# Two graph layers on one core: the first four chunks' source rows gathered from x before the branch, a shorter last chunk, and a rewritten end of layer 1

## The chip, the cores and the metric

The kernel runs on one core of one Trainium2 chip. The metric is the device time of one execution, in microseconds, as the median of several runs; smaller is better. A profile of one execution comes with it: the span from its first to its last instruction, and a trace of every instruction and transfer.

A core has five instruction streams that work side by side. PE is the matrix engine, DVE the vector engine, ACT the scalar engine with its tables of functions, POOL is GpSimd, and SP only issues transfers. Each works through its own instructions in order and waits at semaphores for the others. Transfers are issued by SP, ACT or GpSimd and carried by 16 DMA engines that they share.

## The reference, cut to what matters

There are 12,500 nodes with rows of 128 numbers and 200,000 edges sorted by their target `dst`. Two layers follow one another. Both gather a row per edge by `src` and add up per target node.

```python
# layer 1: attention with 4 heads of 32
loops = jnp.arange(N); src, dst = edges with the loops appended
xl = (x @ W_l).reshape(N, HEADS, C)
xr = (x @ W_r).reshape(N, HEADS, C)
h = xl[src] + xr[dst]
e = jnp.einsum('ehc,hc->eh', jax.nn.leaky_relu(h, NEG_SLOPE), att)
p = jnp.exp(e - segment_max(e, dst)[dst])
alpha = p / segment_sum(p, dst)[dst]
out = segment_sum(alpha[:, :, None] * xl[src], dst).reshape(N, HID) + bias + x
out = layernorm(out) * ln_gamma + ln_beta
x = layernorm(x + out)
# layer 2
m = x[src] + edge_attr_128
h = 2.0 * x + segment_sum(m, dst)
h = h @ W1 + b1
h = jnp.where(h > 0, h, 0.01 * h)
x = layernorm(x + h @ W2 + b2)
```

## The kernel before, in words

Edges are handled in 112 chunks of 1792, laid out as 128 partitions by T = 14 edges; a column of 128 edges is called a tile here. The last chunk holds the 1088 edges that are left, laid out in the same 14 columns on 78 partitions. As the edges are sorted, the targets of a chunk lie within 128 consecutive nodes, and a chunk's result is 128 node rows; a row that two chunks share is carried from one to the next.

**Prologue** (lines 49 to 136). The index data are loaded (`dsth`, `n0b`, `srcs`), DVE derives from them what the chunks need (`rel`, `same`, `lastf`, `thru`, `nid`, `khot`) and the flag that says whether the sorted path may be used. In 14 groups of 7 node tiles, PE turns the rows of x (L129) and multiplies them by W_l (L134), and `xl = x @ W_l` is written to DRAM as `xl_d`. Then each engine reads the flag and branches (L138, L139). All that follows is inside the branch.

**Layer 1** (`fast_path`, L215 to L601) is written out by hand: under `manual_schedule` the order of the calls is the order on each engine. Iteration c of the loop at L512 holds pieces of four chunks at once: the loads of chunk c+2 (`load0`), the gather and node work of chunk c+1 (`gather`, `nodes1` to `nodes3`, `parts2`, `parts3`, `node_by_edge`), the attention scores of chunk c (`products`, `leaky`, `scores`, `weights0`, `weights1`), the weights, messages and sums of chunk c-1 (`weights2` to `weights6`, `edge_by_node0`, `messages`, `sums`), the merge with the row carried over for chunk c-2 (`merge1`, `merge2`), and the carry of chunk c-3. The two layer norms work on pairs of chunks: `norm1a` and `roots` in odd iterations, `norm1b` and `norm2` in even ones; `norm2` stores the finished rows to `x1_d` (L500). Two more iterations and four more calls after the loop bring the last chunks to their end.

`gather` (L179) issues one indirect transfer per tile on GpSimd:

```python
got = pool.tile([P, T, D], F32, name="got", bufs=4)
...
nc.gpsimd.indirect_dma_start(out=got[:n, t, :], in_=table[:N, :], in_offset=...srcs[:n, c, t:t + 1]...)
```

It reads `xl_d` in layer 1 and `x1_d` in layer 2. There are four buffers, so gather c+1 waits until the messages of chunk c-3, the last readers of its buffer, are through. `products` turns the gathered rows (L302) and adds the target's part (L305); `messages` reads them again (L403).

**Layer 2** (L604 to L693) loads the edge features (`load1`), gathers from `x1_d`, builds a 0/1 matrix on ACT (`edges1`, L198, L199) and multiplies it with both (`sums1`, L633, L634); `finish1` does the dense part and the last norm for up to four chunks and stores the rows.

## Time and profile before

| | us |
|---|---|
| median of 3 runs (4065.29 to 4066.28) | 4066.21 |
| the profiled execution | 4072.12 |
| its span, first to last instruction | 4070.3 |
| PE busy | 3228.6 (79%) |
| GpSimd busy, 3136 gathers (L186) and 5 others | 2991.6 (73%) |
| DVE busy | 1820.0 (45%) |
| ACT busy | 1825.0 (45%) |
| mean granted clock of PE | 0.781 |

On the page, a row of digits shows an engine's busy share in 40 equal slices of the span, in tenths. A group's line gives the line of the kernel, the engine, the operation, what it writes and reads, how often, then its busy time and the mean length of one, then the idle time of the engine just ahead of it and what ended most of it; "issue" means that nothing in the trace was waited for. In a list of waits the columns are the total, the number of times and the longest. A timeline line gives the start and length in us. "POOLq" and "SPq" are the sequencers that issue.

### The profile page before, as it was taken

Reading aid. Unit: us, or ns where it says so; the run is one execution under the profiler, and the core shown is the slowest. Engines: PE = TensorE matmul, PEld = TensorE weight load, DVE = VectorE, ACT = ScalarE, POOL = GpSimd, SP = SyncE. Lnnn points to the kernel's source line nnn. Section 1 sums busy time; section 2 is a strip of 40 time slices with the busy share of each in tenths; the row PEclk is TensorE's granted clock in tenths of the full one; section 3 lists DMA queues with packets and bytes.
Section 4 is the critical chain, followed back from the end, with each engine's and each line's share of the span. In section 5 each row is a group of like instructions: output and inputs, shape, how many; then the busy total and the mean of one; then the engine's idle time right before and its main releaser. Section 6 shows DMA issues by size and latency. Waiting matters only on the chain. (4 is left out here: it accounts for less than half of the span.)

```text
span 4070.3 us, 55444 instructions
## 1 busy us (share of the span) xinstructions
PE 3228.6 (79%) x18162; PEld 2678.9 (66%) x18274; DVE 1820.0 (45%) x6070; ACT 1825.0 (45%) x4382; POOL 2991.6 (73%) x3141
## 2 busy tenths in 40 slices
PE   6988989999898988989857677767767776677776
PEld 5777777777777777777755555555555555555555
DVE  3778787887878878778730101010101001010101
ACT  2555555555555555555543433333333434333332
POOL 2777777777777777777747777777777777777776
PEclk8888887888888888888876777777777777767777
DMA  6334343333334334334323433333333333333332
GB/s 209 105 111 115 115 115 105 115 115 105 114 115 115 115 105 115 110 111 115 103 79 100 121 101 112 110 112 109 95 118 101 121 100 117 105 112 110 102 111 70
DMA packets 236135, 451.21 MB, mean 111 GB/s; under 512 B 66104, under 2 KB 124601, under 8 KB 235836
## 3 DMA queue, kind: packets, MB, share of 16 engines
q0 software_dynamic: 100384, 205.04, 19.4%
q1 hardware_dynamic: 134876, 240.68, 17.6%
q8 instruction: 147, 2.41, 0.2%
q10 hardware_dynamic: 576, 1.84, 0.1%
q14 instruction: 152, 1.25, 0.1%
HBM read 426.22 MB, written 21.10 MB: 110 GB/s over the span
## 5 line engine op out<-in xcount | busy, mean ns | idle before, releaser
L186 POOL DMA_INDIRECT got<-xl_d,srcs x1568 | 1501.9, 958 | 540.9 <-issue 488.4
L186 POOL DMA_INDIRECT got<-x_d,srcs x1568 | 1488.5, 949 | 521.1 <-issue 468.0
L634 PE MATMUL ps<-got,od 128*128 128x128 f32 x3136 | 858.2, 365 | 433.5 <-DMA got<-x_d,srcs 428.1
L634 PEld LDWEIGHTS ps<-got,od 128*128 128x128 f32 x3136 | 629.6, 249 | 578.8 <-DMA got<-x_d,srcs 575.5
L633 PE MATMUL ps<-ea,od 128*128 128x128 f32 x3136 | 782.3, 341 | 18.3 <-DMA ea<-in_edge_attr 18.3
L639 DVE SCALAR_TENSOR_TENSOR h<-x1w,ps 128x128 f32<-128x128 f32 x112 | 32.2, 287 | 1560.0 <-PE ps L634 1560.0
L633 PEld LDWEIGHTS ps<-ea,od 128*128 128x128 f32 x3136 | 640.4, 253 | 44.3 <-issue 25.7
L411 PE MATMUL ps<-val,od 128*128 128x137 f32 x3136 | 586.7, 367 | 6.1 <-DVE val L403 6.1
L411 PEld LDWEIGHTS ps<-val,od 128*128 128x128 f32 x3136 | 568.9, 271 | 6.2 <-issue 5.2
L329 PEld LDWEIGHTS sc<-attm,lk 128*128 128x128 f32 x3136 | 443.3, 213 | 86.5 <-DVE lk L313 65.1
L198 ACT ACTIVATE od<-iota,nrel 128x128 f32<-128x128 f32 x1568 | 479.9, 387 | 0.0
L329 PE MATMUL sc<-attm,lk 128*128 128x4 f32 x3136 | 446.8, 263 | 23.4 <-DVE lk L313 12.2
L644 ACT COPY ns<-ps 128x128 f32<-128x128 f32 x111 | 29.5, 266 | 950.8 <-DVE h L639 950.8
L312 ACT ACTIVATE lk<-ph 128x512 f32<-128x512 f32 x448 | 242.7, 542 | 356.6 <-PE ph L305 355.2
L313 DVE TENSOR_TENSOR lk<-ph,lk 128x512 f32<-128x512 f32 x448 | 278.3, 621 | 231.1 <-ACT lk L312 229.4
L305 PE MATMUL ph<-odt,parts 128*128 128x512 bf16 (+1 forms) x1232 | 320.2, 366 | 7.9 <-ACT odt L295 1.7
L302 PE MATMUL ph<-ident,got 128*128 128x128 f32 x1568 | 279.1, 290 | 48.0 <-DMA got<-xl_d,srcs 47.3
L319 DVE TENSOR_TENSOR od<-bank,rel 128x512 f32<-128x512 f32 x448 | 272.1, 608 | 60.7 <-PE ps L411 60.6
L403 DVE TENSOR_TENSOR val<-got,bank 128x512 f32<-128x512 f32 x448 | 274.0, 613 | 0.9 <-issue 0.5
L302 PEld LDWEIGHTS ph<-ident,got 128*128 128x128 f32 x1568 | 198.8, 155 | 108.9 <-DMA got<-xl_d,srcs 54.3
L293 ACT ACTIVATE odt<-row,nnid 128x1024 bf16<-128x1024 int32 x224 | 233.6, 1043 | 0.0
L199 ACT ACTIVATE od<-od 128x896 f32<-128x896 f32 x224 | 212.7, 949 | 7.1
(142 smaller groups left out, 3253.8 us busy)
## 6 DMA issues: line engine op xcount, KB each, us to landing
ea<-in_edge_attr SPq DMA_DIRECT2D x111, 896.0 KB
row<-in_dst_rows SPq DMA_DIRECT2D x336, 256.0 KB
got<-xl_d,srcs POOLq DMA_INDIRECT x1568
got<-x_d,srcs POOLq DMA_INDIRECT x1568
row<-in_dst_rows SPq DMA_DIRECT2D x112, 128.0 KB
xg<-in_x_pad SPq DMA_DIRECT2D x112, 64.0 KB
x_d<-x1w SPq DMA_DIRECT2D x112, 64.0 KB
out<-y SPq DMA_DIRECT2D x111, 64.0 KB
```

Of the source, the lines that this page charges most:

```text
L186: nc.gpsimd.indirect_dma_start(out=got[:n, t, :], out_offset=None, in_=table[:N, :], in_offset=bass.IndirectOffsetOnAxis(ap=srcs[:n, c, t: ...
L198: nc.scalar.activation(od[:, t, :], iota[:, 0, :], AF.Abs, bias=nrel[:, c, t:t + 1])
L302: nc.tensor.matmul(ph[:, t * P:(t + 1) * P], got[:, t0 + t, :], ident, start=(t == 0), stop=False, is_transpose=True)
L305: nc.tensor.matmul(ph[:, :m * P], parts[:, k, :], odt[:, t0 * P:(t0 + m) * P], start=False, stop=(k == 2))
L312: nc.scalar.mul(lk[:, :m * P], ph[:, :m * P], 0.2)
L313: nc.vector.tensor_max(lk[:, :m * P], ph[:, :m * P], lk[:, :m * P])
L319: nc.vector.tensor_tensor(live["od", c][:, t0:t0 + m, :], bank[:, None, :P].to_broadcast([P, m, P]), rel[:, c, t0:t0 + m, None].to_broadca ...
L329: nc.tensor.matmul(live["sc", c][:, :, t0 + t], lk[:, t * P:(t + 1) * P], attm, start=True, stop=True)
L403: nc.vector.tensor_mul(vh[:, :, :, :C], live["got", c][:, t0:t0 + m, :].rearrange("p t (h c) -> p t h c", h=H), wts[:, t0:t0 + m, :, None] ...
L411: nc.tensor.matmul(ps, od[:, t, :], v[:, t, :], start=(t == 0), stop=(t == T - 1))
L633: nc.tensor.matmul(ps, od[:, t, :], ea[:, t, :], start=(t == 0), stop=False)
L634: nc.tensor.matmul(ps, od[:, t, :], got[:, t, :], start=False, stop=(t == T - 1))
```

## The change

Six things change; the path that is taken when the flag is 0 is also touched, for memory, and does not run here.

1. Constants `EARLY = 4` and `RING = 6`. The gathered rows live in a ring of six fixed buffers instead of four from a pool. `gather` moves into the prologue's function; chunks 0 to 3 are gathered there, ahead of all else, from x instead of `xl_d`. Their `srcs` columns are loaded first.
2. After the branch, `project` turns those four chunks' rows tile by tile and multiplies them by W_l in place: chunk 0 before the loop, chunks 1 to 3 at the end of iterations 0 to 2.
3. The constants of `fast_path` are loaded in the prologue (`constants`), DVE's preparation is spread over the prologue's groups (`later`), and the prologue's turn and multiply steps are interleaved with one step's distance. The row data of chunks 0 and 1 are loaded in one piece each on ACT's queue.
4. The last chunk has 9 tiles on 121 partitions; `tiles[c]` replaces T in the steps of a chunk.
5. The loop of layer 1 ends with iteration 110. What followed is written out anew in another order, with the 0/1 matrix of the last chunk built on ACT in a free buffer of the ring, `sums` of chunk 110 in two parts, and `norm1a`, `norm1b` and `norm2` of the last pairs partly on GpSimd. The last pair is split into two single chunks.
6. `roots` does not load the exponential's table again at the very end.

```diff
+EARLY = 4
+RING = 6
...
+    tiles = [T] * (NCH - 1) + [-(-(E - (NCH - 1) * CE) // P)]
...
+    nc.scalar.dma_start(srcs[:, :1], src_of[:, :1])
+    nc.scalar.dma_start(srcs[:, 1:EARLY], src_of[:, 1:EARLY])
+    ring = [const.tile([P, T, D], F32, name=f"got{i}") for i in range(EARLY)]
+
+    def gather(table, c):
+        got = ring[c % RING]
+        n = min(P, -(-(E - c * CE) // tiles[c]))
+        if n < P:
+            nc.vector.memset(got[n // 32 * 32:, :tiles[c]], 0.0)
+        for t in range(tiles[c]):
+            nc.gpsimd.indirect_dma_start(
+                out=got[:n, t, :], out_offset=None, in_=table[:N, :],
+                in_offset=bass.IndirectOffsetOnAxis(ap=srcs[:n, c, t:t + 1], axis=0))
+        return got
+
+    for c in range(EARLY):
+        gather(a["x_pad"], c)
...
+        def constants():
+            nc.sync.dma_start(n0i, a["n0_row"])
+            nc.sync.dma_start(iota[:, 0, :], a["c_iota"][:, :P].to_broadcast([P, P]))
...
+        def later(i):
+            if i == 0:
+                nc.vector.tensor_scalar(khot, kd, pcol, None, op0=OP.is_equal)
...
+            elif i == 1:
+                nc.vector.memset(same[:, :, 0:1], 0.0)
+                constants()
+                nc.vector.tensor_tensor(same[:, :, 1:], dstf[:, :, :S - 1], dstf[:, :, 1:],
+                                        op=OP.is_equal)
...
+            elif i == 4:
+                nc.vector.tensor_scalar(nrel, rel, -1.0, -FAR, op0=OP.mult, op1=OP.max)
...
+        turn(*parts[0])
+        for i in range(1, len(parts)):
+            turn(*parts[i])
+            times(*parts[i - 1])
+        times(*parts[-1])
...
+    ring += [cp.tile([P, T, D], F32, name=f"got{i}") for i in range(EARLY, RING)]
...
+        pairs = [(c, 2) for c in range(0, NCH - 2, 2)]
+        pairs += [(c, 1) for c in range(2 * len(pairs), NCH)]
...
+            if c < 2:
+                nc.scalar.dma_start(row, a["dst_rows"][c:c + 1, :].to_broadcast([P, CE]))
...
+        def project(c):
+            got, xTs = live["got", c], {}
+
+            def turn(q):
+                t0, m = quads[c][q]
+                pT = ep.tile([P, 4 * P], F32, name="pm", bufs=2)
+                for t in range(m):
+                    nc.tensor.transpose(pT[:, t * P:(t + 1) * P], got[:, t0 + t, :], ident)
+                xTs[q] = ew.tile([P, 4 * P], F32, name="lk", bufs=3)
+                nc.scalar.copy(xTs[q][:, :m * P], pT[:, :m * P])
+
+            def times(q):
+                t0, m = quads[c][q]
+                pl = ep.tile([P, 4 * P], F32, name="ph", bufs=2)
+                for t in range(m):
+                    nc.tensor.matmul(pl[:, t * P:(t + 1) * P], xTs[q][:, t * P:(t + 1) * P],
+                                     wlr[:, 0, :], start=True, stop=True)
+                nc.vector.tensor_copy(got[:, t0:t0 + m, :].rearrange("p t d -> p (t d)"),
+                                      pl[:, :m * P])
...
         load0(0)
         load0(1)
-        put("got", 0, gather(ew, xl_d, 0))
+        for c in range(EARLY):
+            put("got", c, ring[c])
+        project(0)
         nodes1(0)
         nodes2(0)
+        node_by_edge(0, 0, 0)
+        node_by_edge(0, 0, 1)
         parts2(0)
         parts3(0)
         nodes3(0)
...
-        for c in range(NCH + 2):
+        for c in range(NCH - 1):
...
-            if nxt:
-                put("got", c + 1, gather(ew, xl_d, c + 1))
+            if c + 1 >= EARLY:
+                put("got", c + 1, gather(xl_d, c + 1))
...
+            if c + 1 < EARLY:
+                project(c + 1)
...
+        c, k = NCH - 1, len(pairs) - 1
+        weights2(c - 1)
+        edge_by_node0(c - 1, 0)
+        edge_by_node0(c - 1, 1)
+        carry(c - 3)
+        weights3(c - 1)
+        edge_by_node0(c - 1, 2)
+        products(c, 0)
+        weights4(c - 1)
+        merge1(c - 2)
+        leaky(c, 0)
+        weights5(c - 1)
+        weights6(c - 1)
+        edge_by_node0(c - 1, 3)
+        merge2(c - 2)
+        messages(c - 1, 0)
+        messages(c - 1, 1)
+        products(c, 1)
+        scores(c, 0)
+        leaky(c, 1)
+        messages(c - 1, 2)
+        messages(c - 1, 3)
+        put("od", c, ring[(c + 1) % RING])
+        edge_by_node(live["od", c], c, 0, tiles[c])
+        products(c, 2)
+        scores(c, 1)
+        leaky(c, 2)
+        scores(c, 2)
+        weights0(c)
+        weights1(c)
+        norm1a(k - 2, pool)
+        roots(k - 2)
+        weights2(c)
+        sums(c - 1, 0, 7)
+        weights3(c)
+        weights4(c)
+        sums(c - 1, 7)
+        carry(c - 2)
+        weights5(c)
+        weights6(c)
+        norm1b(k - 2, pool)
+        norm2(k - 3, pool)
+        for q in range(len(quads[c])):
+            messages(c, q)
+        merge1(c - 1)
+        sums(c)
+        merge2(c - 1)
+        carry(c - 1)
+        norm1a(k - 1, pool)
+        merge1(c)
+        roots(k - 1, False)
+        merge2(c)
+        norm1b(k - 1, pool)
+        norm2(k - 2, pool)
+        norm1a(k)
+        roots(k, False)
         norm1b(k)
-        norm2(k - 1)
-        roots(k + 1)
+        norm2(k - 1, pool)
+        roots(k + 1, False)
         norm2(k)
...
-        gots[0] = gather(gw, x1_d, 0)
+        gots[0] = gather(x1_d, 0)
```

## The prediction

> **What bounds the kernel now.** I read the page first (who is busy, what the largest groups wait for), then GpSimd's waits, stage windows, and the timeline at the seams.

> ```profile
> POOL 2777777777777777777747777777777777777776
> L186 POOL DMA_INDIRECT got<-xl_d,srcs x1568 | 1501.9, 958 | 540.9 <-issue 488.4
> L186 POOL DMA_INDIRECT got<-x_d,srcs x1568 | 1488.5, 949 | 521.1 <-issue 468.0
> L302 PE MATMUL ph<-ident,got 128*128 128x128 f32 x1568 | 279.1, 290 | 48.0 <-DMA got<-xl_d,srcs 47.3
> ```

> GpSimd issues 3136 gathers, one per tile of 128 edges; nearly all idle before them is "issue", 0.3 us each: it waits for nobody. 1.245 us is the commonest distance between starts. Layer 1's gathers run from 63.81 to 2042.23 and layer 2's from 2086.86 to 4051.88: 1.263 and 1.254 us a gather, 17.68 and 17.56 a chunk of 14. That queue is full except in three places:

> ```profile
> POOL got L186 <- issue: 956.5, 2932, 63.4
> POOL got L186 <- ACT od L198: 43.7, 1, 43.7
> 63.81 1.11 POOL L186 DMA_INDIRECT got<-xl_d,srcs  x1 [63.35 <-issue]
> 2042.23 0.95 POOL L186 DMA_INDIRECT got<-xl_d,srcs  x1 [0.30 <-issue]
> 2086.86 0.96 POOL L186 DMA_INDIRECT got<-x_d,srcs  x1 [43.68 <-ACT od L198]
> ```

> 63.4 us before the first gather (x @ W_l must be in DRAM), 43.7 us between the layers (named after ACT; that is the last finisher seen, the gather needs the last rows of x1_d), and 10.6 us behind the last gather. The rest, 4070.3 - 63.8 - 44.6 - 10.6 = 3951 us, is gathers end to end. So a gain is an earlier first gather, a shorter seam or fewer gathers, provided the compute keeps up.

> Does it? PE is the near rival:

> ```profile
> core 0: us, PE busy (x) PEld busy (x) DVE busy (x) ACT busy (x) POOL busy (x), PEclk, DMA share, GB/s
> 26.00:42.00 16.00, 13.99 (x117) 12.80 (x116) 7.11 (x12) 4.83 (x10) 0.00 (x0) 1.00 0.88 292
> 64.00:80.00 16.00, 2.52 (x7) 1.53 (x7) 1.79 (x12) 0.54 (x2) 12.33 (x13) 0.50 0.66 199
> 904.00:956.50 52.50, 48.72 (x284) 41.66 (x286) 41.35 (x139) 25.43 (x57) 39.71 (x43) 0.78 0.39 113
> 2100.00:2150.00 50.00, 35.42 (x168) 28.61 (x166) 1.42 (x5) 18.77 (x51) 37.81 (x41) 0.73 0.36 108
> ```

> In layer 1 PE is busy over 90% and DVE 79%, in layer 2 only 71% and 3%. The first transpose (L302) of each chunk dates its iteration. Chunks 82 to 85 begin here:

> ```profile
> 1529.95 0.66 PE L302 MATMUL ph<-ident,got 128*128 128x128 f32 x4
> 1546.75 0.66 PE L302 MATMUL ph<-ident,got 128*128 128x128 f32 x4
> 1563.47 0.66 PE L302 MATMUL ph<-ident,got 128*128 128x128 f32 x4
> 1580.19 0.66 PE L302 MATMUL ph<-ident,got 128*128 128x128 f32 x4
> ```

> Over the layer, 83 of 111 iterations last under 18.5 us and average 16.76; most are 16.72, as here. The other 28 last 18.7 to 23.2 and lift the mean to 17.67, the gather's pace. Three or four of 16.7 are followed by a long one: compute catches up with the gather, waits, and then runs part of the iteration on a half clock. I read 16.8 us as the compute's own pace: 0.9 below the gather's. This is the assumption on which most hangs.

> **The change, part by part.**

> *Early gathers.* Chunks 0 to 3 are gathered from x, which needs only srcs. That load now leads ACT's queue (issue at 0.75; dsth, 896 KB, issued there before, landed at 5.4; other early loads at 5 to 8), so the first gather starts at 4 us (3 to 7). 56 gathers x 1.25 = 70. They run beside DVE's preparation, and here a row bears on it:

> ```profile
> 72.74 1.51 POOL L186 DMA_INDIRECT got<-xl_d,srcs  x1 [0.30 <-issue]
> 73.16 0.97 DVE L192 TENSOR_SCALAR nrel<-rel 128x1568 bf16<-128x1568 f32 x1
> ...
> 269.42 1.56 POOL L186 DMA_INDIRECT got<-xl_d,srcs  x1 [0.30 <-issue]
> ...
> 269.41 0.42 DVE L468 TENSOR_TENSOR xb<-xg,L_gnn_ln_beta 128x256 f32<-128x256 f32 x1
> 269.75 0.41 DVE L492 TENSOR_TENSOR x1w<-x1w,L_gnn_ln_gamma 128x256 f32<-128x256 f32 x1
> ```

> Both gathers took 0.6 us over their 0.94: the first beside a DVE tensor_scalar of 0.97, the second beside 1.2 us of adds and products with two SBUF inputs (L468, L492, L493). [...] I take the rows' 5.5 (0 to 12)[...].

> GpSimd then reads the flag and branches. GpSimd shows no price (it idled there); ACT's and PE's read and branch took 0.5 to 1.0 us. I take 1.5 (0.5 to 5). Chunk 4's gather starts at 4 + 70 + 5.5 + 1.5 = 81, where before it starts at 134.55. Its other condition, xl_d complete, is met at about 63.

> *Projection.* What was gathered is x, so `project` turns and multiplies 14 tiles on chip. The prologue does 7 in 0.93 + 1.83 us of PE; 14 are 5.5, with fill 6.3 us, four times, in the PE's order: once before iteration 0, and behind iterations 0, 1, 2. ACT and DVE copies (4 x 0.55, 4 x 0.67) lie beside PE. 25 us of new PE work, not hidden, in the stretch where compute is behind.

> *Prologue and block start.* PE's loop is software-pipelined (3.0 us per 7 tiles, of which PE 2.76), DVE's preparation is spread out: gain up to 4 us. Against it: gathers add 64 KB per 1.25 us (52 GB/s) to 292 GB/s at a DMA share of 0.88, and twelve constant loads move into SP's queue before the branch (12 x 0.43 = 5 us of issue, with up to three x loads in flight as cover). I let the end stand where it is: last xl_d landed and block entered at 63 (57 to 70). Gone from behind the branch: the constants (63.0 to 68.5) and four-piece row loads (68.5 to 75). Then project(0) 6.3, the node work 76.45 to 80.34 (4), ACT's two odt steps ahead of parts2 (2.2): iteration 0 at 75.5, where before it is 80.55.

> *Does the ring hold GpSimd?* Gather c+1 reuses the buffer of c-5, free when messages(c-5) ended, 12.8 us into iteration c-4 (in iteration 110: L302 at 2024.62, last L403 of the chunk ends at 2037.46). Iterations without project: 12.5 for the first (15.0 before, with 3.7 PE idle), 15.5, 16.7; with three projects iteration 3 starts at 75.5 + 44.7 + 18.9 = 139, before 129.5. Gather 8 needs messages(2): 152. GpSimd itself gets there at 81 + 4 x 17.6 = 151.4. So gather 8 starts at 152 instead of 205.4: **53 us** earlier. From there a compute of 16.8 runs away from a gather of 17.6; it catches up around chunk 70, and the layer ends on the gather's pace. What is late next is compute: each us by which iteration 3 slips costs 1 us, and none that it gains is worth anything, as GpSimd's own 151.4 is close behind.

> *Nine tiles.* Chunk 111 has 1088 edges: 9 tiles on 121 partitions instead of 14 on 78. Five gathers fewer in layer 2, all on the path: 5 x 1.254 = **6.3 us**. In layer 1 the five are not worth that: at the seam the work is already on the compute's path, so it is counted in the next step alone.

> *The seam.* From iteration 111's start (2041.71) to layer 2's first gather is 45.1 us. I walked both orders with the durations of the trace, each engine in its order; the old order comes to 45.8, so the walk is good to 1 us. New order: weights1(c) at 12.8 (before 14.0); weights2(c) no longer behind all of sums(c-1); sums(c) 18 matmuls, 3.4 us, ending at 26.8 against 30.1; merge2(c) 32.2 against 33.2; the last pair is split into single chunks, so at the end stand one norm and one store: the old path has four stores of 1.36 in SP's queue (2079.28 + 5.45), the new one a single one behind norm2. Landing 2.1 in both. The walk gives 40.4.

> Norms on GpSimd: the trace has no such operation. From below, DVE's rows (add of 128x256: 0.42). [...] They stand behind the last gather of the layer and delay none; but DVE's stats wait for norm1b's four of them, with messages(c) queued behind the stats[...]. [...] ACT loses table loads (1.28 each). Gain 45.8 - 40.4 = **5.4** (0 to 10).

> *Sum:* 53.4 + 5.4 + 6.3 = 65. The profiled execution has a span of 4070.3 and took 4072.1, 5.9 over the median of the runs; 4072.1 - 65 = 4007 for such a one, **4066.2 - 65 = 4001** for the median.

> **Rivals.** What this kernel's measurement can tell from no change is about 0.2%, 8.1 us.

> *Held at the branch.* Entering the block, each engine waits for what its memory was last used for. If that includes the early gathers, all start at 79 (the last of them landed) instead of 63, iteration 3 at 155, gather 8 at 168: gain 37 + 11.7, 4018. For it: SP and DVE wait at 62.75 for several DMA semaphores in a row. Against: DVE's first instruction waits until 73.02, PE's until 76.45, each for its own data, no common barrier; the ring is not in memory that is reused.

> *PE is the true bound: slower.* The place is layer 1 in full, the price 9.5 us (iteration 3 later than before) plus whatever its pace exceeds 17.7. If iterations of 18.7 to 23.2 are not the echo of a gather wait but a PE that must run at half clock now and then, compute free of the gather still needs 17.67 or more. At 17.9: 139 + 108 x 17.9 = 2072 against 2041.7, so +30 - 5.4 - 6.3 = +19, 4085. It decides from 17.73 us a chunk: (2041.7 + 11.7 - 139) / 108. For it: PE over 90% busy, clock 0.78 in 904 to 956. Against: the runs of 16.72, and waits for gathers just ahead of the long ones. Between 17.15 and 17.7 compute takes part or all of the gain: 4002 to 4063.

> *The early gathers do not overlap*, held to the branch by the order or by a full DMA: 5.4 + 6.3 remain, 4054.

> **How the numbers follow.** Likeliest, the sum: 0.67, own range 3990 to 4012. Held at the branch or a gain otherwise cut to 35 to 50: 0.14, about 4018. Compute takes part: 0.08, of which 0.03 within 8.1 us. No overlap: 0.03. PE the bound, slower: 0.06. A remainder of 0.02 lies within 0.2%. Faster 0.89, same 0.05, slower 0.06. The likeliest range covers start (43 to 60), seam (0 to 10) and norm price; reaching to the branch case, 3986 to 4024.

> **What would show it.** First gather at 3 to 7 us and chunk 4's near 81; gather 8 near 152; layer 2's first gather near 2028 and the last near 3987; the wait between the layers measured from the last gather still about 44, since the gathers end 6 us sooner; L302's waits for got absent in the first half of layer 1 and iterations of 16.7 there. It is wrong if iterations in that half average 17.5 or more, if GpSimd waits for DVE (val L403) far beyond chunk 8, or if the early gathers take much over 1.3 us each.

## The result, and the profile after

The changed kernel takes 4007.87 us (median of four runs, 4003.72 to 4015.32) against 4066.24 for the kernel before on the same chip: a ratio of 0.9857, 95% interval 0.9839 to 0.9874, 58 us less. Measured again beside three of the experiments it took 4006.82 (4004.82 to 4008.02), ratio 0.9850, 0.9835 to 0.9865. The median of all eight runs is 4007.4; differences between experiments are taken to 4006.82 where they ran beside it, else to 4007.4.

The page of after (share of busy time in 40 slices; granted clock of PE in tenths; the three groups that the prediction showed of before):

```profile
POOL 7777777777777777777667777777777777777776
PEclk8888888888888888888867777777777777777777
L69 POOL DMA_INDIRECT got<-x_d,srcs x1563 | 1482.2, 948 | 480.8 <-issue 228.0
L69 POOL DMA_INDIRECT got<-xl_d,srcs x1507 | 1441.4, 956 | 461.7 <-issue 165.5
L352 PE MATMUL ph<-ident,got 128*128 128x128 f32 x1563 | 262.5, 285 | 1.2 <-DMA got<-xl_d,srcs 1.2
```

GpSimd works from the first slice on, where its digit was 2. PE's transposes (L352, before L302) wait 1.2 us for gathered rows in the whole layer, where they waited 47.3. The timeline of GpSimd and PE in after gives the places that the prediction dated (start, duration, instruction, idle before it):

```profile
3.23 1.13 POOL L69 DMA_INDIRECT got<-in_x_pad,srcs  x1 [2.80 <-DMA srcs<-in_src_lay]
11.22 2.68 POOL L69 DMA_INDIRECT got<-in_x_pad,srcs  x1 [0.30 <-issue]
77.61 0.94 POOL L69 DMA_INDIRECT got<-in_x_pad,srcs  x1 [0.30 <-issue]
78.86 0.94 POOL L69 DMA_INDIRECT got<-xl_d,srcs  x1 [0.30 <-issue]
149.51 0.94 POOL L69 DMA_INDIRECT got<-xl_d,srcs  x1 [0.89 <-issue]
152.61 0.95 POOL L69 DMA_INDIRECT got<-xl_d,srcs  x1 [2.15 <-issue]
1980.40 1.24 POOL L69 DMA_INDIRECT got<-xl_d,srcs  x1 [0.30 <-issue]
1983.04 0.66 PE L352 MATMUL ph<-ident,got 128*128 128x128 f32 x4
2026.90 1.07 POOL L69 DMA_INDIRECT got<-x_d,srcs  x1 [4.71 <-DMA x_d<-x1w]
3984.20 0.99 POOL L69 DMA_INDIRECT got<-x_d,srcs  x1 [0.30 <-issue]
```

The 56 early gathers run from 3.23 to 78.86. Between the last of them and the first behind the branch lie the usual 1.25 us: reading the flag and branching cost GpSimd nothing. Chunk 8's gather starts at 149.51 (before 205.44) and the ring then holds its second tile for 1.85 us. Layer 1's last gather starts at 1980.40 (before 2042.23), layer 2's first at 2026.90 (before 2086.86).

PE's stages in after, by the windows shown of before:

```profile
core 0: us, PE busy (x) PEld busy (x) DVE busy (x) ACT busy (x) POOL busy (x), PEclk, DMA share, GB/s
26.00:42.00 16.00, 13.45 (x99) 12.24 (x98) 9.96 (x19) 4.54 (x10) 12.65 (x12) 0.91 0.88 310
64.00:80.00 16.00, 10.17 (x51) 7.34 (x51) 3.90 (x10) 6.93 (x13) 12.14 (x13) 0.69 0.53 187
904.00:956.50 52.50, 46.59 (x307) 38.79 (x307) 41.95 (x144) 28.99 (x65) 40.01 (x42) 0.89 0.38 111
2100.00:2150.00 50.00, 35.53 (x183) 29.19 (x182) 6.14 (x20) 20.07 (x53) 37.81 (x41) 0.74 0.38 112
```

GpSimd is busy beside the prologue, and PE has 10 us of work in the 16 behind the branch where it had 2.5. The windows cut from one L352 to the next show single iterations, here 46, 47, 50 and 51:

```profile
873.29:888.36 15.07, 13.43 (x101) 10.87 (x100) 12.92 (x45) 8.10 (x21) 11.41 (x13) 1.00 0.28 78
888.36:907.57 19.21, 16.54 (x101) 13.83 (x100) 15.13 (x52) 10.98 (x24) 14.39 (x16) 0.82 0.55 161
...
941.75:958.47 16.72, 15.08 (x100) 12.53 (x99) 14.45 (x51) 7.91 (x20) 12.74 (x13) 0.90 0.21 53
958.47:976.37 17.90, 17.74 (x101) 15.46 (x100) 13.67 (x46) 11.10 (x24) 13.55 (x15) 0.71 0.55 163
```

This is the most instructive table of the case. The same 100 or so PE instructions take 15.07 us at the full clock, 16.72 at 0.90, 19.21 at 0.82 and 17.90 at 0.71, with no wait for gathered rows. Each of the 16 iterations of 15.1 us among numbers 8 to 110 is followed by one of 19.1 to 19.3. Over these iterations the mean is 17.07 us and the clock 0.866. What I had read as a compute pace of 16.7, with long iterations as the echo of a gather wait, is one mean over short and long iterations, while the clock goes up and down and no rows are waited for.

What PE does wait for, near the end of an iteration, is DVE's part of the next chunk's node work (`nodes3`, L331), 136.9 us in all:

```profile
L331 PE MATMUL pm<-attm,lks 128*128 128x4 f32 x224 | 51.0, 298 | 136.9 <-DVE sr L313 130.4 <-DVE lks L310 5.6
```

In the trace of after the granted clock is 1.0 or 0.5, and each of its 426 stretches but the one at the trace's end lasts a multiple of 3.413 us; a piece of 3.413 us is called a window here. Between 400 and 1936 us PE was busy for 69% of a full window on average when a half one followed (75 windows), and for 94% when another full one followed (252); each of the 76 half windows that a full one followed was busy throughout. So in this trace the half clock came more often after a window in which PE had waited. Single windows depart from this (47 to 97% busy ahead of a half one, 55 to 100% ahead of a full one), and no run filled the wait to see what the clock does then.

### The profile page after: what moved, and what is told of

The parts are those of the page before. It is cut to its first block, busy times and chain, and to the rows that moved or that the text cites. A ratio compares the mean times of both kernels' runs of the same rounds, so it can differ in the third digit from the quotient of the medians.

```text
span 4001.8 us, 58604 instructions
## 1 busy us (share of the span) xinstructions
PE 3185.4 (80%) x18394; PEld 2636.4 (66%) x18394; DVE 1822.4 (46%) x6074; ACT 1823.0 (46%) x4397; POOL 2994.8 (75%) x3147
## 3 DMA queue, kind: packets, MB, share of 16 engines
q1 hardware_dynamic: 133627, 238.52, 17.7%
## 5 line engine op out<-in xcount | busy, mean ns | idle before, releaser
L69 POOL DMA_INDIRECT got<-xl_d,srcs x1507 | 1441.4, 956 | 461.7 <-issue 165.5
L766 PE MATMUL ps<-ea,od 128*128 128x128 f32 x3126 | 779.0, 340 | 18.5 <-DMA ea<-in_edge_attr 18.5
L467 PEld LDWEIGHTS ps<-val,od 128*128 128x128 f32 x3108 | 556.8, 268 | 0.0
L379 PEld LDWEIGHTS sc<-attm,lk 128*128 128x128 f32 x3126 | 410.9, 202 | 103.5 <-DVE lk L363 90.1
L379 PE MATMUL sc<-attm,lk 128*128 128x4 f32 x3126 | 427.3, 257 | 31.5 <-DVE lk L363 21.1
L362 ACT ACTIVATE lk<-ph 128x512 f32<-128x512 f32 (+1 forms) x447 | 241.8, 541 | 286.6 <-PE ph L355 285.6
L363 DVE TENSOR_TENSOR lk<-ph,lk 128x512 f32<-128x512 f32 (+1 forms) x447 | 277.2, 620 | 176.1 <-ACT lk L362 174.1
L355 PE MATMUL ph<-odt,parts 128*128 128x512 bf16 (+1 forms) x1341 | 334.1, 359 | 1.1 <-ACT odt L345 1.1
L369 DVE TENSOR_TENSOR od<-bank,rel 128x512 f32<-128x512 f32 (+1 forms) x444 | 269.7, 608 | 45.9 <-PE ps L467 45.4
L458 DVE TENSOR_TENSOR val<-got,bank 128x512 f32<-128x512 f32 (+1 forms) x447 | 273.7, 613 | 1.3 <-issue 0.7
L352 PE MATMUL ph<-ident,got 128*128 128x128 f32 x1563 | 262.5, 285 | 1.2 <-DMA got<-xl_d,srcs 1.2
L352 PEld LDWEIGHTS ph<-ident,got 128*128 128x128 f32 x1563 | 192.8, 154 | 49.2 <-PE pm L414 25.6
```

The lines of the kernel that those rows point to most:

```text
L69: nc.gpsimd.indirect_dma_start(out=got[:n, t, :], out_offset=None, in_=table[:N, :], in_offset=bass.IndirectOffsetOnAxis(ap=srcs[:n, c, t: ...
L352: nc.tensor.matmul(ph[:, t * P:(t + 1) * P], got[:, t0 + t, :], ident, start=(t == 0), stop=False, is_transpose=True)
L355: nc.tensor.matmul(ph[:, :m * P], parts[:, k, :], odt[:, t0 * P:(t0 + m) * P], start=False, stop=(k == 2))
L362: nc.scalar.mul(lk[:, :m * P], ph[:, :m * P], 0.2)
L363: nc.vector.tensor_max(lk[:, :m * P], ph[:, :m * P], lk[:, :m * P])
L369: nc.vector.tensor_tensor(live["od", c][:, t0:t0 + m, :], bank[:, None, :P].to_broadcast([P, m, P]), rel[:, c, t0:t0 + m, None].to_broadca ...
```

## The experiments

The theory at the outset: GpSimd's queue of gathers still sets the time, and compute, at 17.07 us an iteration by the clock, arrives at the end of layer 1 just with it. Rivals: compute alone is now the bound; or the own pace is 16.7 and the gathers slow it.

**Early gathers undone, the rest kept.**

```diff
-    for c in range(EARLY):
-        gather(a["x_pad"], c)
...
-            put("got", c, ring[c])
-        project(0)
+            put("got", c, gather(xl_d, c) if c == 0 else ring[c])
...
-            if c + 1 >= EARLY:
-                put("got", c + 1, gather(xl_d, c + 1))
+            put("got", c + 1, gather(xl_d, c + 1))
...
-            if c + 1 < EARLY:
-                project(c + 1)
```

> The early gathers alone are undone: all 112 chunks are gathered from x_l behind the branch and nothing is multiplied on chip; nine tiles, the layer's end and GpSimd's norms stay. Theory (the queue of gathers sets layer 1's end): chunk 0's gather starts at about 63, chunk 4's at 133 where it was 78.9, the layer's last gather near 2034, and the time is 4004 + 54 = 4058 (4050 to 4062), about 8 us under before. Rival (the compute's pace sets the end of layer 1 after the change): with iteration 0 at about 82 and four projections less, iteration 111 comes no later than it did, and the time stays within 10 us of 4004.

4058.33 us (ratio to before 0.9978, 0.9969 to 0.9988). The first gather starts at 66.03, chunk 4's at 136.37, the layer's last at 2036.46. So the early gathers are worth 4058.3 - 4007.4 = 50.9 us, and all else about 9 (4067.4 for before, beside it), although this kernel's first gather starts 2.2 us later than before's 63.81. The rival, a time within 10 us of 4004, falls: without the early gathers, the queue of gathers sets the layer's end.

**Layer 1's gathers left out.**

```diff
-                put("got", c + 1, gather(xl_d, c + 1))
+                put("got", c + 1, ring[(c + 1) % EARLY])
```

> Layer 1's gathers from chunk 4 on are left out; the chunks read what chunks 0 to 3 left in the ring, so the output is not the reference's. Theory (17.07 us an iteration is the compute's own pace, because the granted clock drops to a half for about an eighth of the 3.41 us windows whatever GpSimd does): iterations 8 to 110 still average 16.95 to 17.15, in the repeating steps of 15.1, 16.7, 17.9 and 19.2, clock 0.86 to 0.88 there, iteration 111 within 10 us of 1983. Rival (16.7 is the own pace, as the prediction took it, and gathering beside it costs 0.3 us an iteration): they average 16.7 to 16.8, iteration 111 near 1945, and the time falls by 35 to 40 us.

4005.55 us (3998.35 to 4012.02): with 1507 of 3126 gathers gone, the time is the same. Iterations 8 to 110 average 17.06, the clock there is 0.866, iteration 111 starts at 1988.67. (Its profiled execution, 4012.02 us, was the slowest of four, and its iteration 3 starts at 144.17, 5.9 later than in after; why is not known. The half clock holds in 28% of the windows from 400 to 1936 us; the eighth of the expectation is what it takes off the mean.) Compute alone needs as long as compute and gathers together; 16.7 was never its pace.

**Projection left out**, `project(0)` and `project(c + 1)` deleted.

> The four multiplications of gathered rows by W_l on chip are left out (chunks 0 to 3 then carry x where x_l belongs, so the output is not the reference's); all else stays. Compute is then 19 to 25 us further on at iteration 3 and has slack up to the layer's end. Theory (compute catches up with the gathers only at the very end, so their small differences reach the time): the wait of the ring at chunk 8 goes (1.85 us) and iteration 111 stands by its rows when they land, so the stretch from the layer's last gather to the next layer's first one falls from 46.5 to 40 to 44: time 3995 to 4002, and the runs lie closer together than the 11.6 us of the changed kernel. Rival (the gathers alone set the end): 46.5 stays and the time falls by no more than 2 us.

4002.42 us (4000.43 to 4005.82), 5.0 under the changed kernel, with ranges that overlap by 2 us. Compute now has slack and waits for rows:

```profile
L352 PE MATMUL ph<-ident,got 128*128 128x128 f32 x1563 | 265.8, 287 | 8.2 <-DMA got<-xl_d,srcs 8.2
```

The ring's wait at chunk 8 is gone. The last gather starts at 1978.58, where the changed kernel has 1980.40 and, in a second profile told of below, 1978.29; the stretch behind it is 46.65, beside 46.51 and 51.18. So it did not fall to 44, and that part of the theory is not borne out. Layer 2's first gather comes 1.7 and 4.2 us sooner than in those two (2025.23 against 2026.90 and 2029.47). Together with the run before: compute alone gives about 4005, and gathers with compute ahead of them about 4002. In the changed kernel compute sets layer 1's pace, as PE waits 1.2 us for rows in all, and the gathers stand within 5 us behind it: two bounds close together.

**Three early chunks**, `EARLY = 3`.

> EARLY = 3 instead of 4. Chunk 3's gather then needs x_l in DRAM and the branch (62 to 64) where the third chunk's gathers end at about 61.4, so GpSimd loses 1 to 3 us; one projection of 6.3 us and the wait of the ring at chunk 8 (1.85) go. Theory (compute is the tighter of the two at the layer's end): the last gather stays within 1.5 us of 1980.4, the stretch behind it falls by 2 to 5 us: 3998 to 4003. Rival (the gathers alone set the end): 4003 to 4006.

4014.11 us (4010.43 to 4016.81), 6.7 slower; neither expectation held. GpSimd's timeline has the place:

```profile
61.08 0.94 POOL L69 DMA_INDIRECT got<-in_x_pad,srcs  x1 [0.30 <-issue]
69.95 0.94 POOL L69 DMA_INDIRECT got<-xl_d,srcs  x1 [7.92 <-PE pn L299]
```

Chunk 3's gather waits until 69.95, not 62 to 64, beside a PE transpose that itself waits for the load of `xg`. (The buffer of chunk 3 now lies in memory of the block behind the branch as well; which of the two it waits for is not separated.) Chunk 4's starts 8.6 us later than in the first profile of the changed kernel, the last 7.7 later, layer 2's first 6.3 later. Here the later start of the gathers cost nearly all that it was late, and the projection saved (6.3) did not make up for it.

**The changed kernel again.**

> The changed kernel once more, for its spread and as the neighbour of the three below. Theory: 4004 to 4012, median near 4008, and within it the time follows the granted clock as it does in the runs without gathers (0.801: 3998.35, 0.798: 4003.76, 0.797: 4007.33, 0.795: 4012.02). Rival: the seven us over the forecast were chance, and the median comes to about 4002.

4006.82 us. The range of the theory holds; its second half, that the time follows the clock, doesn't: the run with a clock of 0.804 took 4006.17, that with 0.797 took 4004.82. From iteration 111's start to layer 2's first gather this profile has 46.08 us (1983.39 to 2029.47), the first one 43.86. Runs of one kernel differ by 2 us there.

**Fourteen tiles in the last chunk**, its edges laid out on 78 partitions as before.

```diff
-    tiles = [T] * (NCH - 1) + [-(-(E - (NCH - 1) * CE) // P)]
+    tiles = [T] * NCH
...
         leaky(c, 2)
+        products(c, 3)
         scores(c, 2)
+        leaky(c, 3)
+        scores(c, 3)
```

> The last chunk has 14 tiles on 78 partitions again (products, leaky and scores of its fourth quad stand after those of the third); the rest is as changed. Layer 2's five further gathers cost 5 x 1.2525 = 6.3. Theory (at the end of layer 1 compute stands on the path, its five gathers there are hidden): the stretch from iteration 111 to layer 2's first gather grows from 43.9 to 46 to 48, so +8 to +11 in all: about 4017. Rival (layer 1's gathers also count): +12.5 or more, 4020 or above. Third: only layer 2's 6.3 show, 4014.

4021.08 us (4018.76 to 4027.31), 14.3 more than the changed kernel beside it. Layer 1's last gather starts at 1989.26, 8.9 later than in the first profile of after (five gathers are 6.3 of it, and chunk 8 started 2.0 later), and 48.30 us behind it the next layer's starts, within what after shows there (46.51 and 51.18). The rival's number, 12.5 or more, came true. Its reason, that the five gathers count in layer 1 too, is not shown alone: the last chunk also has five tiles more to compute, and from iteration 111's start to layer 2's first gather it is 52.08 us here, beside 43.86 and 46.08 in the two profiles of after. The fourth quad (a group of up to four tiles) was put where I thought best, so part of the 14.3 may be its place: the order of before took 45.15 with its 14 tiles.

**The old order at the end of layer 1**, with nine tiles: the loop's generic steps for c = 111 to 113 in place of the written-out end, chunks 110 and 111 one pair, norms on DVE.

```diff
-        pairs = [(c, 2) for c in range(0, NCH - 2, 2)]
-        pairs += [(c, 1) for c in range(2 * len(pairs), NCH)]
+        pairs = [(c, min(2, NCH - c)) for c in range(0, NCH, 2)]
...
-        for c in range(NCH - 1):
-            prv, old = c > 0, c > 1
+        for c in range(NCH + 2):
+            on, nxt, prv, old = c < NCH, c + 1 < NCH, 0 < c <= NCH, c > 1
...
-        c, k = NCH - 1, len(pairs) - 1
-        dve, pool = nc.vector, nc.gpsimd
...
+        k = len(pairs) - 1
+        norm1b(k)
+        norm2(k - 1)
+        roots(k + 1)
+        norm2(k)
```

> The last three steps of layer 1 in their order of before, with chunks 110 and 111 as one pair and all norms on DVE; early gathers and nine tiles stay. The prediction gives the new order 5.4 us (+5.4, 4013). The changed kernel's own trace gives it 1.3: theory, from iteration 111's start to layer 2's first gather 44.5 to 46 instead of 43.9, +0.5 to +2, not to be told from the changed kernel. Rival: 49 or more, as the walk has it.

4005.46 us (4001.79 to 4007.40), 1.4 under the changed kernel and not to be told from it. PE's and GpSimd's timelines put iteration 111 and layer 2's first gather 42.80 us apart:

```profile
1984.29 0.33 PE L353 MATMUL ph<-ident,got 128*128 128x128 f32 x1
2027.09 0.98 POOL L69 DMA_INDIRECT got<-x_d,srcs  x1 [42.56 <-DMA x_d<-x1w]
```

The new order is worth nothing that can be told; one reason is given below, under the seam. What the stretch lost against before (45.15 with 14 tiles) comes with the nine tiles.

**Norms of the end back on DVE**, `dve, pool = nc.vector, nc.vector`.

> In the new order of layer 1's end every norm is put back on DVE; the order stays. GpSimd took 0.8 to 1.1 us for a tensor_scalar of 128x128 (DVE 0.33) and 0.72 for an add of 128x256 (DVE 0.42). Theory: DVE is the path there, so the norms of pairs k-2 and k-1 (about 2.5 us each on DVE) push messages and merges back, while DVE no longer waits for GpSimd (0.86) : iteration 111 to layer 2's first gather 44 to 47, 0 to +3 in all. Rival (GpSimd's norms are too slow and hold DVE's statistics): 41 to 43, -1 to -3.

4009.34 us (4006.62 to 4019.47), 2.5 over the changed kernel with ranges that overlap; the stretch is 46.66, beside 43.86 and 46.08. Unclear: what GpSimd's norms are worth can't be told from nothing. The rival, that they hold DVE by 1 to 3 us, has nothing for it.

**Less PE work, without layer 1's gathers**: two of the three bf16 products.

```diff
-            for k in range(3):
+            for k in range(2):
...
-                                 start=False, stop=(k == 2))
+                                 start=False, stop=(k == 1))
```

> As the run without layer 1's gathers from chunk 4 on, and in addition only two of the three bf16 products by odt are made for each four tiles (the smallest part of x_r is left out, and the gathered rows are wrong as before). One part costs PE 334 us / 112 / 3 = 1.0 us an iteration. Theory (compute's own pace of 17.06 is PE's work at the clock that it is granted): the pace falls to 15.6 to 16.3, iteration 111 to 1870 to 1915. Rival (DVE, or the chain between the engines, sets 17.06): 16.8 or more.

4007.45 us, where the run with three products took 4005.55. The pace is 17.06 again. The windows from 400 to 1936 us say how, first with three products, then with two (both without gathers):

```profile
400.00:1936.00 1536.00, 1399.09 (x8913) 1171.77 (x8913) 1263.87 (x4278) 848.75 (x1893) 0.00 (x0) 0.86 0.20 63
```

```profile
400.00:1936.00 1536.00, 1440.14 (x8463) 1258.06 (x8552) 1271.83 (x4276) 854.88 (x1891) 0.00 (x0) 0.77 0.20 62
```

361 weight loads fewer (PEld's count), and PE is busy 41 us longer, at a granted clock of 0.77 instead of 0.86. My theory failed: the clock was no constant that PE's work is divided by; with less work it was lower. The rival's number, 16.8 or more, came true; its cause, DVE or the chain between the engines, is neither shown nor excluded. DVE's busy time is the same in both, as that cause would have it. PE's wait for DVE at L331 is shorter with two products (55.7 us from 400 to 1936, beside 106.9), and single iterations of 15.07 at the full clock show that the chain can go faster once, though a long one follows each of them in after.

**The same with all gathers kept.**

> The changed kernel with two of the three bf16 products by odt (the smallest part of x_r left out); all gathers stay. Compute's own pace is then about 16, well under the gathers' 17.6. Theory (in the changed kernel gathers and compute come to the end of layer 1 together; the gathers alone would be there 2 to 5 us sooner): 4000 to 4004, as with no projection (4002.4), the last gather near 1978.5 because the ring's wait at chunk 8 goes. Rival (compute is the bound of layer 1): 3990 or less.

4005.86 us (3999.46 to 4012.32): no change that can be told. Pace 17.06, clock 0.77; iteration 3 starts at 147.54 instead of 138.32, and the ring holds chunk 8 until 158.32. The theory's numbers failed because the edit did not make compute faster.

**The norms' rows in PSUM**, the memory in which this kernel's PE results lie, instead of SBUF, where its rows and gathered data lie. In after, gathers 112 to 1562 last 18.7 us longer than 0.944 each in all. 16.6 of that excess (17.1 as counted in the expectation) is in the 136 gathers that overlap DVE's adds and products of L525, L550 and L551, whose inputs both lie in SBUF: those last 1.066 us on average, the other 1315 last 0.946.

```diff
+        sumx = bank[:, P + T * H:].rearrange("p (n d) -> p n d", n=2)
+        scb = ep.tile([P, T * H + 3 * D], F32, name="scb")
+        prow = {}
+        for i, name in enumerate(("L0_gnn_bias", "L0_gnn_ln_gamma", "L0_gnn_ln_beta")):
+            prow[name] = scb[:, None, T * H + i * D:T * H + (i + 1) * D]
+            nc.vector.tensor_copy(prow[name], rows[name])
...
-            xb = ew.tile([P, 2, D], F32, name="xb")
+            on = eng is nc.vector
+            xb = sumx if on else ew.tile([P, 2, D], F32, name="xb")
```

> The changed kernel with bias, gamma and beta of the first norm, and the sum of x and a row, held in PSUM, so that none of DVE's adds and products of the norms in the loop has both inputs in SBUF; the values are the same. In the changed kernel's trace gathers 112 to 1562 take 18.7 us over 0.944 each in all, 17.1 of it in gathers beside those operations (L525, L550, L551). Theory ([...]compute is the second wall): the excess falls under 4 us and the last gather comes 5 to 15 us sooner where the ring lets it, but iteration 111 is not before 1976, and the time is 4000 to 4006. Rival 1 (the gathers alone set the end): 3988 to 3992. Rival 2 (where an operand lies doesn't matter): the excess and the time stay, 4005 to 4009.

4003.56 us (4002.20 to 4004.97). The excess falls to 6.7. The last chunk's gathers could start 8.75 us sooner, and must wait; GpSimd's, PE's and DVE's timelines of this run:

```profile
1957.13 0.96 POOL L69 DMA_INDIRECT got<-xl_d,srcs  x1 [0.30 <-issue]
1966.85 1.02 POOL L69 DMA_INDIRECT got<-xl_d,srcs  x1 [8.75 <-PE ph L358]
...
1964.98 1.02 DVE L67 MEMSET got<- 32x1152 f32 x1 [0.30 <-issue]
...
1965.90 0.44 PE L358 MATMUL ph<-ident,got 128*128 128x128 f32 x2
...
2026.97 1.07 POOL L69 DMA_INDIRECT got<-x_d,srcs  x1 [4.97 <-DMA x_d<-x1w]
```

Chunk 111 fills 121 partitions; its `got` is cleared from partition 96 on by DVE (L67), queued where iteration 110 begins, and its gathers follow that: GpSimd's sequencer waits for DVE from 1952.24 to 1966.04, where the clearing ends. (The line names L358, merely the last to finish before the gather.) The wait costs nothing here: iteration 110 starts at 1965.90 as it did at 1966.31, and layer 2's first gather at 2026.97 as it did at 2026.90. The gathers are faster, compute is not; that is the second bound seen from its other side. The time is 3.9 us under the changed kernel's eight runs, the best median of all runs with the full computation, but 0.1% of the time, less than can be told safely.

**Both edits.**

> Both edits of the two runs before it: two parts, and the rows in PSUM. Theory (two walls close together: only moving both moves the end): the last gather near 1963, layer 2's first gather near 2009, and the time 3986 to 3993, more than the two gains together. Rival (the two gains add, 3 to 6 us each): 3997 to 4002.

4011.25 us (4009.86 to 4012.28), slower than with the rows in PSUM alone; with two parts alone single runs come to 4012 too. The excess is 3.9, but compute stays at 17.06 with iteration 3 at 149.15, and layer 2's first gather is at 2034.89. Both predictions fall for one reason: fewer products bring no faster compute. Whether moving both bounds would bring the 15 us that the gathers could give (an excess of 18.7 less 3.9) is therefore open. To keep PE busier at the end of an iteration, where it waits for DVE, and see what its clock does then, was not tried.

## Why the prediction was right, and where its steps were off

The forecast was 4001, range 3986 to 4024, faster at 0.89. The time is 4007.4 to 4007.9: the gain is 58 us where 65 were put.

- *Early gathers, 53.4.* The dates hold: first gather 3.23 (4), chunk 4 at 78.86 (81; the 1.5 us for flag and branch were not needed), the excess of the 56 gathers over 0.944 us each, beside DVE's preparation, 5.7 us (5.5), iteration 0 at 74.98 (75.5), iteration 3 at 138.32 (139), chunk 8 at 149.51 (152, held by the ring as foreseen). By experiment 50.9. The 5.5 was an estimate from before's two gathers of 1.51 and 1.56 us: 0.6 of the length of casts and scalars (4.0 us of them in the preparation) and half the length of operations with two inputs (6.3 us). The sum is right, its terms are not. The gathers beside large casts and scalars (starting at 7.18, 26.00 and 33.23; two of them beside copies as well) are 1.5 us over, where 2.4 were put; those beside two compares (L135, L163) are 1.73 and 1.75 us over, nearly the compare's whole length, as here, where the compare takes 1.90:

```profile
11.22 2.68 POOL L69 DMA_INDIRECT got<-in_x_pad,srcs  x1 [0.30 <-issue]
11.18 1.90 DVE L135 TENSOR_TENSOR down<-dstf 128x1680 f32<-128x1680 f32 x1
```

  The other runs with four early chunks have 4.8 to 6.6 us, so the agreement is in part luck.
- *Compute's pace, 16.8.* This is the step that failed, the one "on which most hangs". It is 17.06, by the run without gathers; compute catches up at the layer's last chunk instead of at chunk 70. It cost little only because of where it fell: I had put the point from which compute takes part at 17.15 (from the prediction's own dates it comes to 17.12: 2041.7 less 53.4 and 139, over 108), and 17.06 lies less than 0.1 us under it. That is luck. The mistake was to take the commonest iteration (16.72) for the pace and to explain the long ones away as echoes of waits. In part they were: from iteration 8 on before has 21 that are longer than 19.45 us, after none. (The granted clock was 0.73 on average in before's 28 long iterations, 0.88 in the other 83.) The others stay, with half-clock stretches in them, when the gathers are gone: the clock there is 0.866. The rival *PE is the true bound*, whose PE must run at half clock now and then, had that right and the size wrong; what sets 17.06 is open.
- *Nine tiles, 6.3.* From layer 2's first to its last gather it is 7.7 and 6.2 in the two profiles (1957.3 and 1958.8 against 1965.0). In layer 1 I gave them nothing of their own; the run with 14 tiles puts the two together at 14.3. Not all of that can be theirs: before less the early gathers' 50.9 is 4016.0 us (4066.94 on that chip), so the new order with 14 tiles, at 4021.08, stands 5 us behind the old one.
- *The seam, 5.4.* The walk was right for the old order, and wrong for the new one. Measured 43.86 and 46.08 against 40.4. The old order with nine tiles has 42.80. The walk had a single store behind `norm2` at the end, for four in the order of before. The trace has four in both, one behind the other in SP's queue (before, then after):

```profile
2079.28 5.45 SPq L500 DMA_DIRECT2D x_d<-x1w  x4
2019.49 5.39 SPq L558 DMA_DIRECT2D x_d<-x1w  x4
```

  In after the first is issued when GpSimd has finished a norm of pair k-2, and the last at 2024.54, 1.0 us after the last norm ended (2023.54). From the first of them to layer 2's first gather it is 7.58 us in before, 7.41 in after and 7.58 with the old order and nine tiles: the queue holds the end in all three, and norms that end sooner than it gain nothing. The larger part of the gap, ahead of the last norm, is not taken apart by any run. One term there is GpSimd's `tensor_scalar` of 128x128, for which the prediction has no price: it takes 0.78 to 1.11 us (1.58 for two), DVE's 0.34 at the median. The price of GpSimd's adds in the walk was an estimate that no trace of before shows. Here the add of 128x256 takes 0.71 us, DVE's of before 0.42. In the timeline of after:

```profile
1997.63 1.58 POOL L518 TENSOR_SCALAR x1w<-x1w,mv,sd 128x128 f32<-128x128 f32 x2 [15.15 <-DVE sd L544]
1999.18 0.71 POOL L525 TENSOR_TENSOR xb<-xg,L_gnn_ln_beta 128x256 f32<-128x256 f32 x1
2018.72 0.29 DVE L510 BATCH_NORM_STATS2 st<-x1w 128x6 f32<-128x128 f32 x1 [0.86 <-POOL x1w L551]
```

  DVE waits 0.86 us for GpSimd once. These terms do not explain the whole gap of 3.5 to 5.7 us. The granted clock in the stretch, 0.68 and 0.62 in the two profiles, which the walk did not carry, is a candidate, but not the main one by these runs: the old order took 42.80 at 0.63, and the norms on DVE 46.66 at 0.66.
- *The sum, 65.* The profiled spans differ by 68.5 (4070.3 and 4001.8), but before's profiled run was above its median and after's was the fastest of its four. The medians differ by 58.4. By the runs: early gathers 50.9 for 53.4, all else 9.1 for 11.7, together 60.0. One reading was loose: the 10.6 us behind the last gather end with the last busy instruction; to the end of the span it is 18.4, so the gathers end to end are 3943 us, not 3951. Nothing hangs on it.
- *Rivals.* Not held at the branch: PE's project starts at 61.8, iteration 0 at 74.98. The early gathers overlap. Compute takes part, but with a few microseconds.

## What to carry to other kernels

Before taking a pace from the commonest iteration, cut the trace at iteration starts and read the granted clock of each piece; where long and short pieces hold the same instructions and no wait for their input, the mean is the pace. When one bound is moved until it meets another, moving one alone gains no more than the distance between them: here a run without the gathers and a run without the extra compute each gave the same time within 5 us, and said more than any row. A shorter last chunk was worth more than the reordering written around it, which a single run with the old order would have shown.

## What the runs showed of the hardware

Gathers beside DVE's adds and products with both inputs in SBUF took longer on GpSimd, 1.066 us where the others took 0.946: 18.7 us of excess over 1451 gathers fell to 6.7 when the rows and the sum lay in PSUM, with the same values on the same engine. A second profile of the changed kernel has 16.6.
